# A graph-attention layer: 128 instead of 84 edge groups without gathers, in tiles of 128 consecutive edges, their column one-hots made by ScalarE

## The chip, the core and the metric

The kernel runs on one core of a Trainium2 chip. The metric is device microseconds of one execution; beside it there is one profiled execution, to which all times of single instructions belong. In the profile PE is the matrix engine (PEld its weight loads), DVE the vector engine, ACT the scalar engine (ScalarE), POOL the engine that issues indirect gathers, and SP the queue for most other DMAs.

## The reference, cut to what matters

There are 12500 nodes with 64 features and 400000 edges with 64 features, sorted by destination. Every node takes a softmax over its incoming edges and sums their messages:

```
h_src, h_dst = x[src], x[dst]
e     = leaky_relu(concat[h_src, h_dst, edge] @ W_attn + b_attn, 0.01)
alpha = exp(e - segment_max(e, dst)[dst]) / segment_sum(exp(..), dst)[dst]
z     = segment_sum(alpha * (concat[h_src, edge] @ W_ne), dst)
out   = layernorm(x + relu(concat[x, z] @ W_out))
```

The destination of the edge at place e of the sorted list is about 12500 (e/400000)², so low-numbered nodes have many edges each, and a run of consecutive edges there touches few nodes.

## The kernel before, in words

Because W_ne is linear, the kernel sums alpha-weighted raw features (`acc`, 128 x nodes: 64 rows for edge features, 64 for source features) and multiplies by the weights once per node.

Edges come in 782 groups of 512 (`GE`), a group being 128 partitions x 4 places (`P`, `T`). Edge number 4p + t of a group lies in partition p and place t.

**Main loop** (L717 to L748). Groups 83 to 781 go through batches of 20 groups (`BS`; the last two have 11 and 8), each of chunks of four groups (`SG`). For a chunk, `gather` (L176) loads the edge features with one DMA on SP and the source rows with 16 indirect DMAs on POOL (L191), into one of eight buffers (`ZB`). `scores` (L197) makes the attention scores on DVE; ScalarE copies each chunk's window of destination terms to `win` (L205, one buffer). `softmax` (L271) is a chain of scans and transposes, nearly all on DVE, at whose end ScalarE stores the weights in `fixed` (L354). `aggregate` (L366) weighs one-hots of the destinations (`w`, L369, DVE), multiplies features by them on PE (L377), 64 matmul instructions per chunk, and adds each group's 48-node window to `acc` (L387, DVE). Only when a chunk's matmuls are done is its buffer free for the gathers of a later chunk.

**Dense part** (`dense_part`, L548). The first 84 groups (`KD`), where edges crowd on few nodes, take no gathers. It is a generator: each `yield` ends one *step*, and the main loop calls one step after each chunk's scores and one after every second chunk's aggregation (`i % 2`, L742). The groups come in three dense batches of 32, 28 and 24 (`DENSE`), and for each of these:

- Set-up: two steps. `indices` (L128) loads and transposes sources and destinations (`lo` and `hi` are source modulo 128 and source divided by 128; `drel` the destination relative to the group's first).
- Score steps (L585 to L607), one per group: PE spreads the low source numbers over the partitions, DVE turns them into a one-hot `lot` (L593), PE multiplies it with the table of source scores (L596), and DVE picks with a one-hot of `hi` (L598 to L606).
- The dense softmax (L611) and a step's end.
- Aggregation steps (L621 to L645), one per group. For each of the four places DVE makes `lo_w`, a 128 x 128 one-hot of the low source number times alpha (L628), and `hot_c`, a one-hot of the *code* (node offset x 98 + hi) over 3, 4 or 5 nodes of 98 columns (L631). PE multiplies them into one PSUM tile over the four places (L633) and the edge features by `we` (L636). Then DVE loads a register with the group's offset (L638) and adds the result to `sums` (30 nodes x 98 columns, L642) and to `esum` (L644).
- At the end of a *sub-block* of groups (`subs`): 98 matmuls of x by columns of `sums` (L658) with 25 loads of x, in five pauses, and the add to `acc_d`. There are eight sub-blocks; each begins by clearing `sums` (L618).

`finish` (L508) makes 512 finished output rows. While the dense part runs, it is called only after the aggregation of a chunk that has no step; later in the score loop too. There is also a general path, started when a flag (`odd`, `worst`) says that a window was too narrow; it isn't run for this input.

PSUM tile `pg` has four buffers, which matmul results of the main loop, of the dense part and of `finish` share. Each engine runs its instructions in order; the order is settled when the program is built, and follows the program closely.

Of the kernel before, what the change touches and what calls it, by code (L numbers as in the profile page):

```python
# [9 lines left out]
F32 = mybir.dt.float32  # L10
I32 = mybir.dt.int32
# [4 lines left out]
P = 128  # L16
# [18 lines left out]
DENSE = ((32, 3, (32,)), (28, 4, (10, 9, 9)), (24, 5, (7, 6, 6, 5)))  # L35
KD = 84
ND = 5
NA = 30
NDW = 192
# [7 lines left out]
def sorted_path(ctx, tc, x, dst, idx, edge, w_ne, w_attn, b_attn, w_out, out, flag):  # L47

# [46 lines left out]
    ofs = const.tile([1, KD], I32, name="ofs")  # L95
# [32 lines left out]
    def indices(g0, G, dense=False):  # L128
# [13 lines left out]
        if dense:  # L142
            low = dn.tile([P, T, P], F32, name="lot", bufs=2).bitcast(I32)
            nc.vector.tensor_scalar(low[0:G], raw[0:G].rearrange("g (p c) -> g c p", c=2 * T)[:, 0:T, :],
                                    P - 1, None, op0=OP.bitwise_and)
            lows = chunks.tile([BG, T, P], BF16, name="lows", bufs=1)
            nc.scalar.activation(lows[0:G], low[0:G], AF.Copy)
        nat = raw.bitcast(F32)
# [5 lines left out]
        pp = psum.tile([P, 2 * T, BG], F32, name="pp", bufs=1)  # L154
# [3 lines left out]
        srcs = chunks.tile([P, T, BG], I32, name="srcs_d" if dense else "srcs", bufs=1 if dense else 3)  # L158
# [3 lines left out]
        return (srcs, pp, lows) if dense else (srcs, pp)  # L162

    def slots_of(g0, G, pp, wide=S, name="drel", bufs=3):

        drel = chunks.tile([P, T, BG], F32, name=name, bufs=bufs)
        nc.scalar.activation(drel[:, :, 0:G], pp[:, T:2 * T, 0:G], AF.Copy)
# [103 lines left out]
    def softmax(G, y, d3, carry, first, alpha=alpha, tag=""):  # L271
# [25 lines left out]
        er = rows.tile([P, T, P // T], F32, name="er")  # L297
        nc.vector.transpose(er.rearrange("r t q -> r (t q)"), y.rearrange("p t g -> p (t g)"))
        e = rows.tile([P, P], F32, name="e")
        nc.scalar.activation(e.rearrange("r (q t) -> r q t", t=T), er.rearrange("r t q -> r q t"), AF.Copy)  # L300
# [37 lines left out]
        else:  # L338
# [11 lines left out]
        nc.vector.tensor_tensor(al.rearrange("r t q -> r q t"), ex.rearrange("r (q t) -> r q t", t=T),  # L350
                                sm.rearrange("r (q t) -> r q t", t=T), op=OP.mult)
        alpha0 = rows.tile([P, P], F32, name="b1").rearrange("p (t g) -> p t g", t=T)
        nc.vector.transpose(alpha0.rearrange("p t g -> p (t g)"), al.rearrange("r t q -> r (t q)"))
        nc.scalar.activation(alpha, alpha0, AF.Copy)  # L354
# [77 lines left out]
    with before:  # L432
# [28 lines left out]
        d0f = pre.tile([1, KD], F32, name="d0f", bufs=1)  # L461
        rel = pre.tile([1, KD], F32, name="rel", bufs=1)
        nc.vector.tensor_copy(d0f, d0i[:, 0:KD])
        g0 = 0
        for n in [n for _, _, subs in DENSE for n in subs]:
            nc.vector.tensor_scalar(rel[:, g0:g0 + n], d0f[:, g0:g0 + n], d0f[:, g0:g0 + 1], None, op0=OP.subtract)
            g0 += n
        nc.vector.tensor_reduce(odd[:, 0:1], rel, axis=AX.X, op=OP.max)
        nc.vector.tensor_scalar(odd[:, 0:1], odd[:, 0:1], float(ND - NA), None, op0=OP.add)
        nc.vector.tensor_scalar(rel, rel, 0.0, float(NA - ND), op0=OP.max, op1=OP.min)  # L470
        nc.vector.tensor_copy(ofs, rel)
        nc.vector.tensor_reduce(odd[:, 1:2], d0f, axis=AX.X, op=OP.max)
        nc.vector.tensor_scalar(odd[:, 1:2], odd[:, 1:2], float(NA - NDW), None, op0=OP.add)
        nc.vector.tensor_scalar(d0f, d0f, float(NDW - NA), None, op0=OP.min)
        nc.vector.tensor_copy(at0, d0f)
# [71 lines left out]

    def dense_part():  # L548
# [5 lines left out]
        for G, wide, subs in DENSE:  # L554
            srcs, pp, lows = indices(b0, G, True)
            drel = slots_of(b0, G, pp, wide, "drel_d", 1)
# [8 lines left out]
            code = dn.tile([P, T, BG], F32, name="code")  # L565
            nc.vector.scalar_tensor_tensor(code[:, :, 0:G], drel[:, :, 0:G], float(NB), hi[:, :, 0:G], op0=OP.mult, op1=OP.add)
# [6 lines left out]
            hot = dn.tile([P, T, BG, ND], BF16, name="hot_d")  # L573
            we = dn.tile([P, T, BG, ND], F32, name="we")
            yd = dn.tile([P, T, BG], F32, name="yd")
            sdst = dn.tile([P, T, BG], F32, name="sdst_d")
            for t in range(T):
                nc.vector.tensor_tensor(hot[:, t, 0:G, :], fixed2[:, 0:ND].unsqueeze(1).to_broadcast([P, G, ND]),
                                        drel[:, t, 0:G].unsqueeze(2).to_broadcast([P, G, ND]), op=OP.is_equal)
                nc.vector.tensor_tensor(we[:, t, 0:G, :], hot[:, t, 0:G, :], pw[:, 0:G, :], op=OP.mult)  # L580
            nc.vector.tensor_reduce(sdst[:, :, 0:G], we[:, :, 0:G, :], axis=AX.X, op=OP.add)
# [3 lines left out]
            for g in range(G):  # L585
                ze = dn.tile([P, T, D], F32, name="ze_d", bufs=3)
                nc.sync.dma_start(out=ze.rearrange("p t f -> p (t f)"),
                                  in_=edge[(b0 + g) * GE:(b0 + g + 1) * GE, :].rearrange("(p t) f -> p (t f)", t=T))
# [6 lines left out]
                for t in range(T):  # L595
# [15 lines left out]
            fac, carry = softmax(G, yd, d3, carry, b0 == 0, al, "_d")  # L611
            nc.vector.tensor_tensor(we[:, :, 0:G, :], hot[:, :, 0:G, :],
                                    al[:, :, 0:G].unsqueeze(3).to_broadcast([P, T, G, ND]), op=OP.mult)
            yield
            g1 = 0
            for n in subs:
                sums = dn.tile([P, NA, NB], F32, name="sums")
                nc.vector.memset(sums, 0.0)  # L618
                esum = dn.tile([D, NA], F32, name="esum")
# [592 lines left out]
```

## Time and profile before

| | |
|---|---|
| median of 3 runs | 5798.25 us (5794.36 to 5805.65) |
| profiled execution | 5793.67 us, of which the span 5792.0 |
| busy: PE, PEld | 1926.2 us (33%), 1420.2 us (25%) |
| busy: DVE | 2616.5 us (45%) |
| busy: ACT | 249.9 us (4%) |
| busy: POOL | 2651.7 us (46%) |
| instructions | 47177 |
| DMA | 273.32 MB in 408968 packets, 226448 of them under 512 B |

The profile page gives busy time by engine, a chain of waits followed back from the end, and groups of instructions as "line engine operation output<-input, count | busy us, mean ns of one | idle time before them and what ended it". In waits, "remote" on a single core stands for a matmul whose record is missing, and "issue" is time in which nothing that the profile shows was waited for. A windows view gives for stretches of the span the busy time of each engine with the number of instructions, then the granted PE clock, the DMA share and GB/s. A timeline line is start, duration, engine, line, operation, and in brackets the idle time before it and what ended that.

### The profile page before, as it was taken

The numbers are of one execution on the slowest core, as the hardware profiler recorded it, in microseconds if no ns is written. First come the engines' busy times: TensorE is split into PE (matmuls) and PEld (weight loads), VectorE is DVE, ScalarE is ACT, GpSimd is POOL, SyncE is SP. The second block draws the span as 40 slices with busy tenths as digits, with TensorE's granted clock in tenths as the row PEclk, the third lists the DMA queues.
The fourth block names the chain that finished last, engine by engine and source line by source line (L and its number), as shares of the span: only waits on it lengthen the run. The fifth ranks groups of instructions, "written<-read, shape, count | busy, mean of one in ns | idle before, by whom it ended". The sixth has DMA issues, their size and how long they took to land.

```text
span 5792.0 us, 47177 instructions
## 1 busy us (share of the span) xinstructions
PE 1926.2 (33%) x15668; PEld 1420.2 (25%) x15668; DVE 2616.5 (45%) x7714; ACT 249.9 (4%) x575; POOL 2651.7 (46%) x2811
## 2 busy tenths in 40 slices
PE   0122222233334223232443434423333433344423
PEld 0111222122223222221232322322222322223322
DVE  4434444434554444445544544334446434253435
ACT  0000000000000000000000000000000000000000
POOL 7444444544334555544344455544443455434441
PEclk9855555555555555555655555555555555565555
DMA  7121211111112222211121222212111222212210
GB/s 125 34 45 42 45 42 41 42 42 38 40 39 57 45 48 47 44 45 40 41 60 39 62 45 46 54 46 47 43 42 37 64 45 48 52 42 54 59 42 17
DMA packets 408968, 273.32 MB, mean 47 GB/s; under 512 B 226448, under 2 KB 363196, under 8 KB 408714
## 3 DMA queue, kind: packets, MB, share of 16 engines
q1 hardware_dynamic: 292330, 170.19, 11.4%
q0 software_dynamic: 89696, 93.36, 9.8%
q10 hardware_dynamic: 26688, 6.67, 0.7%
q8 instruction: 125, 2.05, 0.1%
q14 instruction: 129, 1.06, 0.1%
HBM read 263.31 MB, written 9.07 MB: 47 GB/s over the span
## 4 chain that ended last, share of the span: by engine, by line
issue 28%; DVE 26%; another core or an unknown queue 17%; PE 16%; POOL 8%; DMA 3%; DVEq 1%; SPq 1%; ACT 1%; ACTq 0%; POOLq 0%
POOL zx L191 8%; PE pg L377 8%; PE pg L633 4%; DVE prod L223 2%; DVE prod L209 2%; DVE hot L218 2%; DVE sdst L226 2%; DVE row L237 2%; DVE turn L247 2%; DMA ze_d<-in_x_dram 2%; DVE hot_c L631 1%; DVE y L211 1%; PE pg L658 1%; DMA zx<-table,srcs 1%
## 5 line engine op out<-in xcount | busy, mean ns | idle before, releaser
L191 POOL DMA_INDIRECT zx<-table,srcs x2716 | 2565.5, 945 | 2991.9 <-PE pg L377 1973.4
L377 PE MATMUL pg<-w,ze 128*64 128x48 f32 x5592 | 716.4, 291 | 1349.1 <-issue 767.0
L377 PEld LDWEIGHTS pg<-w,ze 128*64 128x64 f32 x5592 | 622.0, 206 | 1426.9 <-issue 1112.1
L377 PE MATMUL pg<-w,zx 128*64 128x48 f32 x5592 | 726.0, 290 | 688.8 <-issue 671.0
L377 PEld LDWEIGHTS pg<-w,zx 128*64 128x64 f32 x5592 | 625.3, 205 | 743.3 <-issue 706.0
L387 DVE TENSOR_TENSOR acc<-acc,pg 128x48 f32 x699 | 137.8, 197 | 1227.8 <-remote 608.4
L633 PE MATMUL pg<-hot_c,lot 128*128 128x294 f32 (+2 forms) x672 | 442.7, 790 | 596.6 <-DVE hot_c L631 428.9
L596 PE MATMUL pg<-ss,lot 128*128 128x98 f32 x672 | 170.3, 435 | 618.0 <-DVE lot L593 382.2
L633 PEld LDWEIGHTS pg<-hot_c,lot 128*128 128x128 f32 x672 | 166.7, 285 | 789.4 <-issue 416.0
L369 DVE TENSOR_TENSOR w<-hot,fixed 128x768 f32<-128x768 bf16 x175 | 162.8, 947 | 409.9 <-remote 273.3
L596 PEld LDWEIGHTS pg<-ss,lot 128*128 128x128 f32 x672 | 149.6, 328 | 660.5 <-DVE lot L593 412.4
L631 DVE TENSOR_SCALAR hot_c<-fixed,code 128x294 f32<-128x294 f32 (+2 forms) x336 | 203.0, 604 | 179.2 <-remote 124.6
L658 PE MATMUL pg<-sums,ze_d 128*64 128x30 f32 x1568 | 188.8, 291 | 137.8 <-DMA ze_d<-in_x_dram 79.8
L205 ACT ACTIVATE win<-wrow 128x192 f32<-128x192 f32 x175 | 58.3, 333 | 3684.4 <-DVE prod L223 3075.7
L211 DVE TENSOR_REDUCE y<-prod 128x16 f32<-128x1024 f32 x175 | 211.3, 1207 | 2.8 <-issue 1.6
L658 PEld LDWEIGHTS pg<-sums,ze_d 128*64 128x64 f32 x1568 | 174.6, 219 | 155.0 <-DMA ze_d<-in_x_dram 82.6
L209 DVE TENSOR_TENSOR prod<-ze,fixed 128x1024 f32<-128x1024 f32 x175 | 211.5, 1208 | 0.0
L642 DVE TENSOR_TENSOR sums<-sums,pg 128x294 f32 (+2 forms) x84 | 46.4, 553 | 323.0 <-remote 207.6
L605 DVE TENSOR_TENSOR sel<-hot_h,pg 128x392 f32<-128x392 bf16 x84 | 47.1, 561 | 295.4 <-remote 245.8
L593 DVE TENSOR_SCALAR lot<-pg,lane 128x512 f32<-128x512 f32 x84 | 62.5, 745 | 239.4 <-remote 238.4
L226 DVE TENSOR_REDUCE sdst<-prod 128x16 f32<-128x768 f32 x175 | 164.7, 941 | 8.4 <-remote 8.2
L223 DVE TENSOR_TENSOR prod<-hot,win 128x768 f32<-128x768 bf16 x175 | 164.9, 942 | 5.1 <-ACT xtt L523 4.9
(212 smaller groups left out, 2388.6 us busy)
## 6 DMA issues: line engine op xcount, KB each, us to landing
ze<-in_edge_dram SPq DMA_DIRECT2D x173, 512.0 KB
zx<-table,srcs POOLq DMA_INDIRECT x2716
ze_d<-in_x_dram SPq DMA_DIRECT2D x192, 128.0 KB
ze_d<-in_edge_dram SPq DMA_DIRECT2D x168, 128.0 KB
wrow<-wins SPq DMA_DIRECT2D x168, 96.0 KB
table<-xt ACTq DMA_DIRECT2D x14, 227.5 KB
xb<-in_x_dram ACTq DMA_DIRECT2D x24, 128.0 KB
out_dram<-sq SPq DMA_DIRECT2D x24, 128.0 KB
```

The source lines that it names most:

```text
L191: nc.gpsimd.indirect_dma_start(out=zx[:, g, t, 0:D] if plain else zx[:, g, t, :], out_offset=None, in_=x[:, :] if plain else table[:, :], ...
L209: nc.vector.tensor_tensor(prod[:, 0:n], ze[:, 0:n], w_edge.unsqueeze(1).to_broadcast([P, n, T, D]), op=OP.mult)
L211: nc.vector.tensor_reduce(yb, prod[:, 0:n], axis=AX.X, op=OP.add)
L223: nc.vector.tensor_tensor(at[:, 0:n], hot[:, 0:n], win[:, 0:n].unsqueeze(2).to_broadcast([P, n, T, S]), op=OP.mult)
L226: nc.vector.tensor_reduce(sdst[:, 0:n], at[:, 0:n], axis=AX.X, op=OP.add)
L369: nc.vector.tensor_tensor(w[:, 0:n], hot[:, 0:n], alpha[:, :, b:b + n].rearrange("p t g -> p g t").unsqueeze(3).to_broadcast([P, n, T, S]) ...
L377: nc.tensor.matmul(pg[at:at + D, g, :], z[:, g, t, 0:D], w[:, g, t, :], start=(t == 0), stop=(t == T - 1))
L387: nc.vector.tensor_tensor(ag, ag, pg[:, g, :], op=OP.add)
L596: nc.tensor.matmul(ps[:, t, :], lot[:, t, :], ss, start=True, stop=True)
L631: nc.vector.tensor_scalar(hot_c[:, 0:wide * NB], fixed2[:, 0:wide * NB], code[:, t, g:g + 1], None, op0=OP.is_equal)
L633: nc.tensor.matmul(pa[:, 0:wide * NB], lo_w[:, t, :], hot_c[:, 0:wide * NB], start=(t == 0), stop=(t == T - 1))
L658: nc.tensor.matmul(pf[D:P, 0:NA], xb[:, j, :], sums[:, :, c0 + j], start=(c0 + j == 0), stop=(c0 + j == NB - 1))
```

## The change

- The dense part takes 128 groups rather than 84, in four dense batches of 32; the main loop keeps 655 groups (before 699) in batches of 16, then 31 of 20, then 11 and 8. The dense accumulator covers 392 nodes rather than 192. There are 16 sub-blocks rather than 8.
- In the dense part a tile (place t) now holds 128 consecutive edges: edge number 128 t + p. Its nodes span at most 2 (first two batches) or 3. Each tile has its own offset into `sums` (`ofs` has 4 per group). The loads of the edge features go in pieces of 256 bytes instead of 1024.
- `hot_c` is 2 x 98 or 3 x 98 wide, and ScalarE makes it in two activations: the distance |column − code|, then relu(1 − distance).
- Each tile has its own matmul result and its own add into `sums`: four adds of 196 or 294 columns per group rather than one of 294, 392 or 490. Four registers are loaded per group rather than one. `we` is made per group in two small DVE operations instead of once per dense batch.
- The dense softmax turns its 128 x 128 blocks with PE instead of DVE and copies.
- A sub-block's 98 matmuls have two pauses rather than five.
- The main loop calls a dense step after every chunk's aggregation rather than after every second, and in the score loop one extra step at every fourth; so `finish` isn't called while the dense part runs.

The diff, cut to its core:

```diff
-DENSE = ((32, 3, (32,)), (28, 4, (10, 9, 9)), (24, 5, (7, 6, 6, 5)))
-KD = 84
-ND = 5
+DENSE = ((32, 2, (32,)), (32, 2, (13, 10, 9)), (32, 3, (7, 7, 6, 6, 6)), (32, 3, (5, 5, 5, 5, 4, 4, 4)))
+KD = 128
+ND = 8
+NT = 3
 NA = 30
-NDW = 192
+NDW = 392
...
-    ofs = const.tile([1, KD], I32, name="ofs")
+    ofs = const.tile([1, KD * T], I32, name="ofs")
...
+        if tiles:
+            pe = psum.tile([P, SG, P], F32, name="pg", bufs=4)[:, 0, :]
+            nc.tensor.transpose(pe, y.rearrange("p t g -> p (t g)"), ident)
+            nc.scalar.activation(e, pe, AF.Copy)
...
+            nc.vector.tensor_scalar(code[:, :, 0:G], code[:, :, 0:G], -1.0, None, op0=OP.mult)
...
-                nc.sync.dma_start(out=ze.rearrange("p t f -> p (t f)"),
-                                  in_=edge[(b0 + g) * GE:(b0 + g + 1) * GE, :].rearrange("(p t) f -> p (t f)", t=T))
+                nc.sync.dma_start(out=ze, in_=edge[(b0 + g) * GE:(b0 + g + 1) * GE, :].rearrange("(t p) f -> p t f", p=P))
...
                 for g in range(g1, g1 + n):
...
+                    we = dn.tile([P, T, ND], F32, name="we")
+                    nc.vector.tensor_tensor(we, fixed2[:, 0:ND].unsqueeze(1).to_broadcast([P, T, ND]),
+                                            drel[:, :, g:g + 1].to_broadcast([P, T, ND]), op=OP.is_equal)
+                    nc.vector.tensor_tensor(we, we, al[:, :, g:g + 1].to_broadcast([P, T, ND]), op=OP.mult)
+                    _, vs = nc.values_load_multi_w_load_instructions(
+                        ofs[0:1, (b0 + g) * T:(b0 + g + 1) * T], engines=(EngineType.DVE,), min_val=0, max_val=NA - NT,
...
                     for t in range(T):
                         nc.vector.tensor_scalar(lo_w[:, t, :], fixed2[:, 0:P], lo[:, t, g:g + 1], al[:, t, g:g + 1],
                                                 op0=OP.is_equal, op1=OP.mult)
-                        hot_c = dn.tile([P, ND * NB], F32, name="hot_c", bufs=2)
-                        nc.vector.tensor_scalar(hot_c[:, 0:wide * NB], fixed2[:, 0:wide * NB], code[:, t, g:g + 1], None,
-                                                op0=OP.is_equal)
-                        nc.tensor.matmul(pa[:, 0:wide * NB], lo_w[:, t, :], hot_c[:, 0:wide * NB],
-                                         start=(t == 0), stop=(t == T - 1))
+                        hot_c = dn.tile([P, NT * NB], F32, name="hot_c", bufs=2)
+                        nc.scalar.activation(hot_c[:, 0:wide * NB], fixed2[:, 0:wide * NB], AF.Abs, bias=code[:, t, g:g + 1])
+                        nc.scalar.activation(hot_c[:, 0:wide * NB], hot_c[:, 0:wide * NB], AF.Relu, bias=one_col, scale=-1.0)
+                        pa = psum.tile([P, 512], F32, name="pg", bufs=4)
+                        nc.tensor.matmul(pa[:, 0:wide * NB], lo_w[:, t, :], hot_c[:, 0:wide * NB], start=True, stop=True)
...
+                        part = sums[:, ds(vs[t], wide), :]
+                        nc.vector.tensor_tensor(part, part, pa[:, 0:wide * NB].rearrange("l (d h) -> l d h", h=NB), op=OP.add)
...
-                    if c0 % (5 * NBC) == 4 * NBC:
+                    if c0 // NBC in (8, 16):
                         yield
...
-        def step():
-            if next(rest, done) is done:
-                return False
+        def step(n):
+            for _ in range(n):
+                if next(rest, done) is done:
+                    return False
             return True
...
                 if k and running:
-                    running = step()
                     steps += 1
+                    running = step(1 + (steps % 4 == 0))
...
-                if k and running and i % 2:
-                    running = step()
-                    steps += 1
+                if k and running:
+                    running = step(1)
```

## The prediction

> **What bounds the kernel now.** I read the page first, then the chain and the waits, then the moment at which each batch's softmax weights are stored, and last the windows between two such moments.
>
> ```profile
> PE 1926.2 (33%) x15668; PEld 1420.2 (25%) x15668; DVE 2616.5 (45%) x7714; ACT 249.9 (4%) x575; POOL 2651.7 (46%) x2811
> ...
> issue 28%; DVE 26%; another core or an unknown queue 17%; PE 16%; POOL 8%; DMA 3%; DVEq 1%; SPq 1%; ACT 1%; ACTq 0%; POOLq 0%
> ...
> L191 POOL DMA_INDIRECT zx<-table,srcs x2716 | 2565.5, 945 | 2991.9 <-PE pg L377 1973.4
> ```
>
> No engine is half busy, so stages alternate. POOL's gathers wait 1973 us for the aggregation's matmuls to free buffers. The stores of the weights give the length of a batch (start and duration come first in each line):
>
> ```profile
> 530.79 0.28 ACT L354 ACTIVATE fixed<-b 128x128 f32<-128x128 f32 x1 [9.96 <-DVE fac L363]
> 689.45 0.28 ACT L354 ACTIVATE fixed<-b 128x128 f32<-128x128 f32 x1 [9.97 <-DVE fac L363]
> 1188.66 0.28 ACT L354 ACTIVATE fixed<-b 128x128 f32<-128x128 f32 x1 [9.37 <-DVE fac L363]
> 1362.88 0.28 ACT L354 ACTIVATE fixed<-b 128x128 f32<-128x128 f32 x1 [9.96 <-DVE fac L363]
> 1885.95 0.28 ACT L354 ACTIVATE fixed<-b 128x128 f32<-128x128 f32 x1 [6.28 <-DVE fac L363]
> 2026.78 0.28 ACT L354 ACTIVATE fixed<-b 128x128 f32<-128x128 f32 x1 [9.97 <-DVE fac L363]
> ```
>
> The first pair holds seven dense score steps: 158.7 us. The second holds seven dense aggregation steps: 174.2. The third holds only light steps (x matmuls, set-up): 140.8. Of the seven steps, five lie in the score loop and two between the chunks of the aggregation. The windows show which of them cost time (length, then busy us of PE, PEld, DVE, ACT, POOL with their counts):
>
> ```profile
> 531.80:634.80 103.00, 26.91 (x339) 22.97 (x339) 19.65 (x55) 0.33 (x1) 63.44 (x68) 0.55 0.23 51
> 634.80:670.00 35.20, 12.28 (x44) 9.30 (x44) 33.94 (x69) 1.34 (x4) 12.11 (x13) 0.50 0.24 43
> ...
> 1189.40:1295.00 105.60, 34.15 (x352) 25.59 (x352) 19.16 (x57) 0.33 (x1) 63.25 (x67) 0.55 0.23 49
> 1295.00:1341.00 46.00, 23.98 (x70) 13.00 (x70) 38.22 (x84) 1.34 (x4) 12.28 (x13) 0.57 0.16 33
> ...
> 1886.60:1988.00 101.40, 34.23 (x342) 28.11 (x342) 23.22 (x59) 3.13 (x6) 63.02 (x67) 0.53 0.23 49
> ```
>
> Lines 1, 3 and 5 are aggregation phases: 101 to 106 us whatever lies in them, DVE 19 to 23 us busy. Lines 2 and 4 are score phases: DVE is busy 96% and 83% of them, and every step there lengthens the batch. The aggregation phase follows the gathers:
>
> ```profile
> 4504.26 0.94 POOL L191 DMA_INDIRECT zx<-table,srcs  x1 [3.39 <-PE pg L633]
> ...
> 4527.16 0.94 POOL L191 DMA_INDIRECT zx<-table,srcs  x1 [3.24 <-remote]
> ...
> 4550.09 0.95 POOL L191 DMA_INDIRECT zx<-table,srcs  x1 [3.25 <-remote]
> ```
>
> A chunk's 16 gathers take some 20 us (23 us from one to the next, less the gap), and 3.2 to 3.4 us after them the next chunk's buffer comes free, with or without a dense step between. So a dense step in the aggregation phase has been nearly free, one in the score loop has its price in DVE time.
>
> **The change part by part.** The base is the profiled execution, 5793.67 us (span 5792.0 and 1.7 around it), 4.6 under the median of 5798.25.
>
> *Batches.* 44 groups leave the main loop (699 to 655): 34 batches of 20 become 31 of 20 and a first of 16, and the two short ones stay. Counted from the first weights to the last short batches there are 31 full periods rather than 33: 2 x 141 (the light pair) = −282. The first batch's four groups are a fifth of a batch, twice: one chunk less before the first weights (224 us in; about −20) and one less in its aggregation (−20): −40.
>
> *Where steps fall.* Counting the loop's calls: in score phases 59 score, 62 aggregation and 33 light steps become 68, 75 and 21; in aggregation phases 25, 22 and 15 become 60, 53 and 27. A fit through the 33 periods gives 3.4 us per score step, 5.6 per aggregation step, 4.7 per light step, 13 per dense softmax and 2.7 per output block (`finish`) in a score phase, with 5.7 us of scatter. A score step keeps its DVE work (0.745 + 0.414 + 0.412 + 0.159 + 0.554 + 0.561 + 0.552 = 3.4 us, the same as its price): 9 x 3.4 = +31.
>
> *The aggregation step.* DVE before: four `lo_w` at 0.398, four `hot_c` at 0.513 to 0.713 (mean 0.604), one add of 0.553, the edge add 0.144: 4.70 us, and a load of one register at 0.31. After: four `lo_w` 1.59; four adds of 196 or 294 columns, which are 0.36 by the slope of the rows 0.461/0.562/0.664 and 0.461, so 1.43 or 1.84; two small `we` operations, taken as twice 0.19 from the 48-column add's 0.197; edge add 0.145: 3.55 or 3.96 us. Its load fetches four registers rather than one; the main loop's load of four takes 0.965. So DVE falls from 5.0 to 4.5–4.9; besides, the one-hots leave a queue that was full. I take 4.9 instead of 5.6 per step, bounds 4.1 (all of the removed `hot_c`, less the adds) and 6.5 (each add waits for its own matmul). 75 x 4.9 − 62 x 5.6 = +20.
>
> *ScalarE.* Each tile has two activations. Widths 192 and 256 take 0.334 and 0.384 us here, so 196 and 294 are about 0.34 and 0.42: 2.7 to 3.4 us for a step, some eleven steps in a batch, 30 to 37 us of 170. Hidden while DVE's own 3.6 to 4 us a step last longer; if the cover goes, the price is R3's. The 43 table loads in this trace (1.283 us each) belong to exponentials and roots; I add none.
> The Trainium skill ("ScalarE: Activation LUTs", What ACT_TABLE_LOAD costs) speaks against this: an activation whose bias is a pointer takes 280 ns + 0.833 ns per element, estimated from it 0.44 and 0.53 us, a pair 0.89 to 1.05, against DVE's 0.51 to 0.71. No row here has such a bias. A step would then be bounded by ScalarE at 3.5 to 4.2 us and I would drop the −0.7 per step: 5720 would be about 5770.
>
> *Sub-blocks* go from 8 to 16, so twice the 98 matmuls and the 25 loads of x, but two pauses instead of five: 33 matmuls per step rather than 20. 21 x 4.7 x 1.65 − 33 x 4.7 = +8. The 2.5 us clear of `sums` is in these steps. *Dense softmax:* 4 rather than 3, +13; the two transposes go from DVE to PE, taken at nothing among a chain of 18 us of DVE work (0.9 of a phase of 20); bound 0 to +1 each.
>
> *Output blocks.* 24 of them come out along the way or at the end. With a step after every chunk none is made while the dense part runs; 13 then fall into score phases, where before they hid in aggregation phases. 13 at 4.5 (2.7 by the fit; 6.3 by the bare end of the kernel; middle) less 2 at 2.7: +53. Three more in the short batches and seven rather than two after the last: +43 with 6.3 each less what the tail hides.
>
> *Edge loads* in 256-byte instead of 1024-byte pieces: SP's queue issues as many loads, three buffers ahead. q1's 292330 packets took 11.4% of 16 engines, 36 ns each; a load of 512 packets is 1.2 us over 16 engines, against 20 us between steps. The 110,000 added packets raise the DMA share by 4 points on 23%. Hidden, 0; bound +0.3 us a step, +90.
> The skill ("DMA: Bandwidth & Descriptors", Specifications) asks for 512 bytes or more for line rate and so speaks against it. A doubled packet time would still be 2.4 us a load, and the sum would not move.
>
> *Stretch of the aggregation phases.* Five steps lie there rather than two, each a chain DVE–PE–DVE in DVE's queue ahead of the next chunk's `w`, and PE's matmuls for it stand before the next chunk's. 3 more aggregation steps are 48 matmuls, 3 score steps 27. Lines 1 and 3 above differ by 13 matmuls and 2.6 us: 0.2 us each, so at most 10 and 5 us a batch; the other batches with aggregation steps last 102 to 104, which gives 0.04 and 2 us. I take 2.9 a batch, nearer the many: 28 batches, +81. Bounds 0 and +280 (the chain of waits no longer hidden at all).
>
> Sum: −282 − 40 + 31 + 20 + 8 + 13 + 53 + 43 = −154, so 5640 with the aggregation phases unchanged; +81 is 5720. Against the median shown this is −1.4%.
>
> **Rivals.**
> R1, the aggregation phases stretch: the place is the gap before a chunk's first gather, 3.3 us now, which becomes 5 or more. Against it: gaps do not differ with and without a step. For it: two steps in a row with matmuls while PE waits 1438 us for "issue". It decides from (5794 − 5640)/28 = 5.5 us a batch; at ten it gives 5920.
> R2, the phases hold wholly and the aggregation step falls to its DVE time (4.3): 5640 − 75 x 0.6 = 5595.
> R3, ScalarE in order: `win` (0.33 us) waits for DVE's L223 (3075.7 us over the run, harmless so far); now up to five tiles' one-hots stand behind it, and the adds and matmuls wait for these. One wait of 2.2 us (pair 0.8, matmul 0.7, hand-overs) per aggregation step in score phases: 75 x 2.2, on 5720, gives 5885.
> R4, the change does not do what it says: a tile with more than 2 or 3 nodes sets the flag that starts the general path. Destinations follow 12500 (e/400000)², at edge 65536 1.3 nodes per 128 edges; tiles of 2 and 3 hold for this input. Thousands of us if wrong.
>
> **How the numbers follow.** Forecast as summed 0.38, R2 0.16, no change 0.05, R1 0.24, R3 0.16, R4 0.01. Faster: 0.54; the runs of before differ by 0.2%, which is what can be told from no change. The likeliest case alone spans 5660 to 5785; with R2's lower bounds (finishes at 2.7, step at 4.1) 5560 and R1 and R3 5940.
>
> **What would show it.** Periods near 166 with score steps and 175 with aggregation steps, 31 of them; aggregation phases of 103 to 108 us, gaps of 3.3 to 4; ACT busy some 640 us (250 now, and 64 x 4 x 0.68 + 64 x 4 x 0.84 for the pairs); a pair 0.68 to 0.84 us. Wrong, if aggregation phases exceed 109 us, if DVE's adds wait for ScalarE's one-hots in the score phases, or if the periods without dense steps exceed 155 because of the output blocks.

## The result and the profile after

The changed kernel takes 6014.5 us (median of 4 runs, 6009.27 to 6016.66) against 5796.3 (4 runs, 5778.7 to 5805.65): 1.038 times before, 95% interval 1.035 to 1.041. The forecast was 5720, range 5560 to 5940. Faster was forecast and it came out slower, outside the range. The profiled execution took 6009.27 us.

The page of the changed kernel, lines that answer those of before:

```profile
PE 2414.2 (40%) x17650; PEld 1801.5 (30%) x17650; DVE 2749.5 (46%) x8457; ACT 684.8 (11%) x1554; POOL 2492.2 (41%) x2635
...
DVE 23%; issue 22%; PE 20%; another core or an unknown queue 18%; POOL 8%; DMA 5%; ACT 3%; DVEq 1%; SPq 1%; ACTq 0%; POOLq 0%
...
L214 POOL DMA_INDIRECT zx<-table,srcs x2556 | 2418.1, 946 | 3319.9 <-PE pg L412 2310.4
...
L697 PE MATMUL pg<-sums,ze_d 128*64 128x30 f32 x3136 | 388.3, 291 | 357.1 <-DMA ze_d<-in_x_dram 257.3
```

160 of these gathers are gone (147 us of POOL's busy time), and so are 16 of the first batch's, which read `x` itself and are listed apart: 176, four for each of 44 groups. But POOL waits 2310 us instead of 1973 for the aggregation's matmuls. PE has 13% more matmul records, and those of x double from 1568 to 3136.

Two of the changed kernel's phases with aggregation steps, then a pair around the end of a sub-block (windows; length, then busy us and counts of PE, PEld, DVE, ACT, POOL):

```profile
872.30:975.90 103.60, 47.75 (x387) 35.77 (x388) 30.27 (x97) 16.21 (x37) 62.76 (x67) 0.52 0.21 53
975.90:1055.30 79.40, 33.69 (x110) 19.74 (x110) 54.34 (x189) 26.62 (x65) 12.90 (x14) 0.50 0.11 24
2127.00:2252.00 125.00, 55.89 (x534) 47.13 (x534) 34.17 (x81) 4.07 (x11) 61.96 (x66) 0.52 0.28 65
2252.00:2325.00 73.00, 36.38 (x117) 21.27 (x117) 43.05 (x170) 28.13 (x68) 13.69 (x15) 0.52 0.13 29
```

The first is an aggregation phase (from the weights' store to the last add into `acc`) with dense steps between all chunks: 103.6 us, no longer than before (102 to 106). The second, the scores and softmax after it, has grown to 79.4 us from 68, and DVE is idle for a third of it. The third line is an aggregation phase that holds the 98 x matmuls of a sub-block: 125 us, 534 matmul records. The fourth is the score phase behind it.

Where the steps really fall is seen by counting `lo_w` (four per aggregation step) in the same two stretches, here for that line alone (length, DVE busy, count, clock, DMA share, GB/s). Changed kernel:

```profile
872.30:975.90 103.60, 7.25 (x19) 0.52 0.21 53
975.90:1055.30 79.40, 11.49 (x29) 0.50 0.11 24
```

Kernel before:

```profile
1188.90:1295.00 106.10, 2.02 (x5) 0.55 0.22 49
1295.00:1363.00 68.00, 9.10 (x23) 0.58 0.12 26
```

In the changed kernel's score loop and softmax there are 29, that is 7.25 steps, where the loop's calls there are 6. The fifth step of the aggregation loop is called after the last chunk, so nothing of the phase is left to hide it. Before, 23 (5.75 steps) where 5 were called.

What DVE waits for in such a score loop (976 to 1035 us; engine, tile and line; waited for; us in total, times, longest):

```profile
PEld pg L675 <- ACT hot_c L673: 33.0, 19, 5.3
ACT hot_c L672 <- DVE lot L668: 28.2, 14, 6.2
DVE sums L681 <- PE pg L675: 9.6, 8, 2.7
DVE sums L681 <- PE pg L678: 5.4, 5, 1.5
```

ScalarE's Abs waits for DVE's `lo_w`, PE for ScalarE's Relu, and DVE's add into `sums` for PE. With two smaller entries DVE waits 19 us there before its adds; in the score loop of before (1295 to 1341 us) it is 7.

### The profile page after: what moved, and what is told of

Its sections match the earlier page's. It is cut to its first block, busy times and chain, and to the rows that moved or that the text cites. A ratio compares the mean times of both kernels' runs of the same rounds, so it can differ in the third digit from the quotient of the medians.

```text
span 6007.6 us, 54654 instructions
## 1 busy us (share of the span) xinstructions
PE 2414.2 (40%) x17650; PEld 1801.5 (30%) x17650; DVE 2749.5 (46%) x8457; ACT 684.8 (11%) x1554; POOL 2492.2 (41%) x2635
## 3 DMA queue, kind: packets, MB, share of 16 engines
q14 instruction: 154, 1.25, 0.1%
## 4 chain that ended last, share of the span: by engine, by line
DVE 23%; issue 22%; PE 20%; another core or an unknown queue 18%; POOL 8%; DMA 5%; ACT 3%; DVEq 1%; SPq 1%; ACTq 0%; POOLq 0%
POOL zx L214 8%; PE pg L412 7%; PE pg L675 5%; DMA ze_d<-in_x_dram 3%; PE pg L697 3%; DVE lot L668 1%; PE pg L678 1%; DVE prod L232 1%; DVE prod L246 1%; ACT hot_c L672 1%; DVE hot L241 1%; ACT hot_c L673 1%; DVE row L260 1%; DVE turn L270 1%
## 5 line engine op out<-in xcount | busy, mean ns | idle before, releaser
L214 POOL DMA_INDIRECT zx<-table,srcs x2556 | 2418.1, 946 | 3319.9 <-PE pg L412 2310.4
L675 PE MATMUL pg<-hot_c,lot 128*128 128x196 f32 (+1 forms) x1024 | 569.1, 668 | 441.7 <-ACT hot_c L673 316.3
L633 PE MATMUL pg<-ss,lot 128*128 128x98 f32 x1024 | 259.5, 434 | 750.4 <-DVE lot L630 686.4
L697 PE MATMUL pg<-sums,ze_d 128*64 128x30 f32 x3136 | 388.3, 291 | 357.1 <-DMA ze_d<-in_x_dram 257.3
L697 PEld LDWEIGHTS pg<-sums,ze_d 128*64 128x64 f32 x3136 | 355.4, 220 | 414.5 <-DMA ze_d<-in_x_dram 282.3
L675 PEld LDWEIGHTS pg<-hot_c,lot 128*128 128x128 f32 x1024 | 251.3, 302 | 660.0 <-ACT hot_c L673 530.7
L672 ACT ACTIVATE hot_c<-fixed,code 128x196 f32<-128x196 f32 (+1 forms) x512 | 238.3, 465 | 1748.0 <-DVE lot L668 1055.4
L681 DVE TENSOR_TENSOR sums<-sums,pg 128x196 f32 (+1 forms) x512 | 208.7, 408 | 286.8 <-PE pg L675 123.4
L668 DVE TENSOR_SCALAR lot<-fixed,lo,al_d 128x128 f32<-128x128 f32 x512 | 204.5, 399 | 196.0 <-ACT hot_c L672 160.6
L673 ACT ACTIVATE hot_c<-hot_c,one_col 128x196 f32<-128x196 f32 (+1 forms) x512 | 255.4, 499 | 16.0
```

Of the source, the lines that this page charges most:

```text
L214: nc.gpsimd.indirect_dma_start(out=zx[:, g, t, 0:D] if plain else zx[:, g, t, :], out_offset=None, in_=x[:, :] if plain else table[:, :], ...
L633: nc.tensor.matmul(ps[:, t, :], lot[:, t, :], ss, start=True, stop=True)
L668: nc.vector.tensor_scalar(lo_w[:, t, :], fixed2[:, 0:P], lo[:, t, g:g + 1], al[:, t, g:g + 1], op0=OP.is_equal, op1=OP.mult)
L672: nc.scalar.activation(hot_c[:, 0:wide * NB], fixed2[:, 0:wide * NB], AF.Abs, bias=code[:, t, g:g + 1])
L673: nc.scalar.activation(hot_c[:, 0:wide * NB], hot_c[:, 0:wide * NB], AF.Relu, bias=one_col, scale=-1.0)
L675: nc.tensor.matmul(pa[:, 0:wide * NB], lo_w[:, t, :], hot_c[:, 0:wide * NB], start=True, stop=True)
```

## The experiments

The recorded pair and e13 to e15 ran under a condition in which the kernel before takes 5800 us; in all other runs it takes 3600 us and the changed one 3923. The expectations speak of two chips. The record doesn't show that: the chip with number 3 stands for runs of both kinds (e1 to e8 and e16 to e18 at 3600, e13 to e15 at 5800), number 1 for e9 to e12 at 3600. Whether it is another chip or another condition of one is open. Times are therefore given as ratios to before beside it, and each experiment says what it can tell of which condition. I call them the 5800 runs and the 3600 runs.

**The two kernels in the 3600 runs (e5, e9).** No edit.

> The changed kernel itself, on the chip of these runs, beside the kernel before. The four experiments so far ran on a chip where the kernel before takes 3600 us instead of 5796, so it must be told what the changed kernel takes beside it. If the chip only scales things: 1.038 times before, some 3735 where before is 3600. But with the own column copy the ratio was 1.053, with 24 of 25 x loads left out 1.099: if both removed something, the changed kernel lies above them, 1.08 to 1.12 times before (3890 to 4030 where before is 3600). Where before is near 5800: 1.035 to 1.042.

3923.4 us against 3599.3: 1.090 (1.088 to 1.092). The loss is more than twice as large there.

> The kernel before, unchanged, to have its profile on the chip of these experiments. If that chip has PE free of the waits for 'issue' during gathers (1438 us in the first profile of before), its aggregation phases last 25 to 60 us instead of 102, and the score phases with softmax the same 55 (score steps) and 68 us (aggregation steps) as in the first profile; DVE is then over 70% busy and bounds the kernel.

3597 us. PE's matmuls wait 67 us for "issue" instead of 1438, the aggregation phases last 22 to 45 us, and DVE is 74% busy. DVE was expected to bound the kernel. But what bounds many batches is POOL, in this window of before (one batch; the last pair is POOL) and in the chain:

```profile
531.80:631.80 100.00, 30.03 (x391) 25.51 (x391) 73.10 (x207) 4.38 (x12) 75.72 (x80) 0.57 0.33 69
```

```profile
POOL 38%; DVE 23%; issue 18%; PE 12%; DMA 7%; ACT 1%; DVEq 1%; SPq 0%; POOLq 0%; ACTq 0%
```

```profile
699.98 0.94 POOL L191 DMA_INDIRECT zx<-table,srcs  x1 [0.30 <-issue]
701.23 0.94 POOL L191 DMA_INDIRECT zx<-table,srcs  x1 [0.30 <-issue]
```

80 gathers, one every 1.25 us, are exactly a batch's 100 us. By its weights' stores the changed kernel's batches with score steps last mostly 115 us there in the first half of the run and 95 to 98 in the second, those with aggregation steps alone 121 to 126: where eleven steps make a batch longer than 100 us, POOL no longer bounds it.

**ScalarE's reading of a tile that DVE reads too (e1, e15).** In the changed kernel's program every Abs waits for DVE and 383 of the 512 `lo_w` for ScalarE, though neither writes what the other reads; both read the PSUM tile `fixed2`. e1 and e15 give ScalarE a copy of its own in SBUF.

```diff
+    cols = const.tile([P, NT * NB], F32, name="cols")
...
-                        nc.scalar.activation(hot_c[:, 0:wide * NB], fixed2[:, 0:wide * NB], AF.Abs, bias=code[:, t, g:g + 1])
+                        nc.scalar.activation(hot_c[:, 0:wide * NB], cols[:, 0:wide * NB], AF.Abs, bias=code[:, t, g:g + 1])
```

> The changed kernel, but ScalarE reads the column numbers for its distances from a copy of its own in SBUF instead of from the PSUM tile fixed2, which DVE reads for lo_w. In the changed kernel's program each Abs waits for DVE and each lo_w for ScalarE, and in the trace each Abs starts 0.1 us after a lo_w ends. Theory A (this hand-over between the two readers of one PSUM tile is what made an aggregation step in the score loop 6.9 us instead of the 4.9 forecast): 75 such steps give back 1 to 2 us each, 5860 to 5940 us. Rival B (two activations of 0.46 and 0.50 us per tile with two buffers are the limit themselves): less than 30 us, 5985 to 6015. Rival C (the add after each tile's own matmul is the limit): also under 30 us.

3788.0 us, 1.053 (1.051 to 1.054): 135 us faster than the changed kernel (3923). The waits of the changed kernel (e5) and of e1 (engine, tile and line; waited for; us in total, times, longest):

```profile
ACT hot_c L672 <- DVE lot L668: 649.4, 338, 28.5
PEld pg L675 <- ACT hot_c L673: 594.6, 403, 3.2
```

```profile
ACT hot_c L676 <- PE pg L679: 611.3, 334, 19.2
...
PEld pg L679 <- ACT hot_c L677: 191.7, 165, 1.9
```

ScalarE no longer waits for `lo_w` but for the matmul that frees a buffer, ahead of time, and PE waits a third as long for it. Aggregation phases with five steps fall from 50 to 31 us, score phases with six from 75 to 68. In e1's program no `lo_w` waits for ScalarE. The instructions themselves got no shorter (`lo_w` 0.40 us in both, Abs 0.42 and 0.51 from PSUM, 0.45 and 0.54 from the copy), so the reading of the tile was not the cost; the order was. The hand-over is shown for the 3600 runs.

> The changed kernel with ScalarE's own column copy once more, in case the runs land on a chip like that of the first pair (before near 5800). There the aggregation phases last 100 us and hide what lies in them, so only the 75 aggregation steps of the score loop gain: 6.9 to about 5.9 us, 60 to 110 us, 5900 to 5955 (1.018 to 1.028 times before). Where before is 3600: 3788 again, 1.053.

In a 5800 run: 6050.4 us, 1.044 (1.041 to 1.046), not faster than the changed kernel's 1.038. The expectation fell. Score phases with six aggregation steps called are 76.6 instead of 79.5 us, so the copy saves 3 us in each, but the 13 periods with ends of sub-blocks are 40 us longer in sum (2546 against 2506). In these periods, but for 3 us, DVE waits for `win`, ScalarE's copy of a chunk's window. First the changed kernel, then e15, whole runs:

```profile
DVE prod L246 <- ACT win L228: 49.7, 6, 13.7
DVE prod L247 <- ACT win L229: 90.2, 9, 18.9
```

That is 41 us more; before there was none. In e15 at 2216 us, for instance, `win` stands in ScalarE's queue behind a one-hot that waits 19.4 us for PE, while PE is at the x matmuls and waits up to 6.7 us at a time for loads of x; DVE waits 14.9 us for that `win`. No run takes this wait away alone.

**One-hots on DVE again (e2).**

```diff
-                        nc.scalar.activation(hot_c[:, 0:wide * NB], fixed2[:, 0:wide * NB], AF.Abs, bias=code[:, t, g:g + 1])
-                        nc.scalar.activation(hot_c[:, 0:wide * NB], hot_c[:, 0:wide * NB], AF.Relu, bias=one_col, scale=-1.0)
+                        nc.vector.tensor_scalar(hot_c[:, 0:wide * NB], fixed2[:, 0:wide * NB], code[:, t, g:g + 1], None,
+                                                op0=OP.is_equal)
```

> The changed kernel with hot_c made by DVE in one comparison again (196 or 294 columns, about 0.42 and 0.51 us by the rows of before), nothing on ScalarE. DVE gets 512 x 0.46 = 236 us more work, some 60% of it under the aggregation phases' idle time. Theory A or B (ScalarE's way of making them costs more than it saves): same or faster than the changed kernel, 5930 to 6010. If ScalarE did save what was forecast (1.85 us per step in the score loop, 75 steps): 6100 to 6150.

4007.8, 1.114 (1.112 to 1.116): 84 us slower than with ScalarE, even with its hand-over. So ScalarE's part does save in the 3600 runs, 84 us as made and 220 with its own copy; theories A and B expected the contrary. The saving that was forecast for DVE, 1.85 us in 75 steps or 139 us, lies between.

**Loads of x and matmuls of x at the sub-blocks' ends (e3, e17, e4, e16, e8).** e3 loads x once per sub-block into a buffer of the edge loads; e17 once for all into a place of its own; both keep the 98 matmuls. e4 and e16 keep 4 of 98 matmuls.

```diff
e17:
-                    xb = dn.tile([P, T, D], F32, name="ze_d", bufs=3)
...
-                        nc.tensor.matmul(pf[D:P, 0:NA], xb[:, j, :], sums[:, :, c0 + j],
+                        nc.tensor.matmul(pf[D:P, 0:NA], xone[:, j, :], sums[:, :, c0 + j],
e4:
                 for c0 in range(0, NB, NBC):
+                    if c0:
+                        if c0 // NBC in (8, 16):
+                            yield
+                        continue
```

> The changed kernel, but each sub-block loads x once (128 KB) and uses that tile in all of its 98 matmuls: 24 of 25 loads are left out (the numbers of the dense nodes' source part are then not those of the layer), the matmuls stay. In the changed kernel 16 sub-blocks lengthen their batches by some 340 us in all. Theory D (the loads are it: PE waits 540 us before these matmuls for x, and SP's queue and DVE's tail memset wait with it): 200 to 320 us faster, 5700 to 5810. Rival E (392 more PE instructions in a row are it, whatever feeds them): under 80 us, 5930 to 6010.

3949.7, 1.099 (1.096 to 1.101): 26 us slower. A buffer held through the matmuls is taken from the edge loads, which may cost something; hence e17.

> The changed kernel with all 98 x matmuls per sub-block, all of them on one tile of x loaded once at the start into a place of its own: no x loads at all (the dense nodes' source part is then not that of the layer), and unlike in e3 no buffer of the edge loads is held. Theory D (the loads, with SP's queue and PE waiting for them, are most of a sub-block's end): most of e16's gain, 150 to 280 us where before is 5796, 80 to 130 where it is 3600. Rival E (PE's 196 matmul instructions in a row are): under a third of e16's gain.

3962.7, 1.101 (1.099 to 1.103): 39 us slower without any load of x. In the 3600 runs the loads are not the cost; theory D fell there. Its trace shows a wait that moved: DVE's add into `acc_d` at a sub-block's end waits 177 us (15 times) for the last x matmul, 18 in e5; in e3 it is 184. That this is why both are slower was not tested.

> The changed kernel with only the first 4 of each sub-block's 98 blocks of x loaded and multiplied; the other loads and matmuls are left out (the dense nodes' source part is incomplete). It prices the sub-blocks' ends whole: theory D and rival E both 260 to 340 us faster than the changed kernel, 5675 to 5755. If it gains under 100 us, the sub-block batches are long for another reason.

3781.0, 1.051 (1.049 to 1.054): 142 us faster. With e17 this leaves PE's 196 matmul instructions per sub-block, and what waits for them, as the cost: 9 us for each of the 16 sub-blocks.

> The changed kernel with 4 of 98 blocks of x per sub-block, as in e4 (the dense nodes' source part is incomplete), once more for the chip on which before takes 5796. By the periods of the changed kernel's profile there, batches with sub-blocks are 344 us longer than their other steps explain: 250 to 340 us faster than the changed kernel's 6014, 0.98 to 0.995 times before. If the sub-blocks' ends are not what makes these batches long: under 120 us, above 1.015 times before. Where before is 3600: 1.051 times before again.

This run too was a 3600 run: 3783.7, 1.051. What the sub-blocks cost in the 5800 runs is thus read from periods only.

> The changed kernel, with the last two 128-row blocks of x kept in a tile of their own from the start: the memset for the partial block, which stands in DVE's queue and waits for a buffer that TensorE frees (193 us of DVE waiting in the profile of the changed kernel, 15 times, up to 26 us), and one load per sub-block fall away. If DVE's wait is what the sub-blocks cost: 100 to 190 us faster than the changed kernel. If x loads and matmuls themselves are it: under 40 us.

```diff
+                    if c0 + NBC > NFULL:
+                        xb = xlast
```

3911.9, 1.086: 11 us faster. DVE's wait for the partial block's memset (193 us in the first profile of the changed kernel, 74 in e5) is nearly all idle time that costs nothing here.

**Both together (e12).** Own column copy and 4 of 98 blocks of x.

> The changed kernel with the own column copy and only the first 4 of each sub-block's 98 blocks of x (the rest of the loads and matmuls left out; the source part of the dense nodes is incomplete). Alone the two gave 135 and 142 us where before is 3600. If they are separate costs they add: 1.013 times before, 3630 to 3670. If both remove the same stall (PE's queue in which both stand): 3720 to 3780.

3633.1, 1.010 (1.008 to 1.012): 290 us, the sum 135 + 142 and 13 more. In the 3600 runs these two are separate costs and 90% of the loss of 324.

**The form of the tiles alone (e6, e18, e7, e11).** The extent and the pacing of before.

```diff
-DENSE = ((32, 2, (32,)), (32, 2, (13, 10, 9)), (32, 3, (7, 7, 6, 6, 6)), (32, 3, (5, 5, 5, 5, 4, 4, 4)))
-KD = 128
+DENSE = ((32, 2, (32,)), (28, 2, (10, 9, 9)), (24, 3, (7, 6, 6, 5)))
+KD = 84
...
-                    running = step(1 + (steps % 4 == 0))
+                    running = step(1)
...
-                if k and running:
+                if k and running and i % 2:
e11, on e7:
-                        hot_c = dn.tile([P, NT * NB], F32, name="hot_c", bufs=2)
+                        hot_c = dn.tile([P, NT * NB], F32, name="hot_c", bufs=3)
```

> The new tiles (128 consecutive edges, ScalarE's one-hots, an add per tile) with the extent of before: 84 groups in dense batches of 32, 28 and 24, eight sub-blocks with five pauses, one step after every score part and after every second aggregation. Only the form of the dense work is changed against before. Theory A (the aggregation step has become about 0.8 us dearer instead of 0.7 cheaper by hand-overs): 62 steps in the score loop, +20 to +80 us on before. My forecast's step (0.7 cheaper): -40 us. If this alone gives the whole loss, the 44 further groups cost nothing; if it gives under a third of it, the loss is in the larger extent (sub-blocks, pacing).

3683.1, 1.023 (1.022 to 1.025). The new form costs 84 us of the 324 without any more groups, about a quarter; by its expectation the rest lies in the larger extent.

> As the run before it (84 groups, new tiles), with ScalarE reading the column numbers from its own copy. Theory A: 1.0 us less per aggregation step in the score loop (six in a row went from 74 to 68 us with it on the fast chip), 60 us faster than the run before it and 0 to 60 us faster than the kernel before. Rival B or C: no difference between the two runs beyond 15 us.

3635.8, 1.010 (1.008 to 1.012): 47 us less, still 37 slower than before, where as fast or faster was expected. One batch holds more than that: the one with the second dense softmax lasts 157 us against 106 before (98.4 + 58.7 against 44.5 + 61.7). In it DVE stands 53.9 us, its longest wait of this kind in e7:

```profile
DVE srcs L183 <- DMA zx<-table,srcs: 140.5, 5, 53.9
```

It is the cast of a later batch's source numbers into `srcs`, a tile that gathers still read. In sum it waits there 75 us in before, 237 in the changed kernel and 268 in e1; no run takes it away, so what it costs is not known.

> 84 groups, new tiles, ScalarE's own column copy, and three hot_c buffers instead of two. In the trace of the changed kernel with the own copy ScalarE's Abs waits 611 us for PE's matmul to free a buffer. If that wait is on the path: 15 to 50 us faster than with two (3636 where before is 3600). If the add after each matmul is the path: within 8 us.

3632.5: 3 us. The wait for a `hot_c` buffer is not on the path of this kernel.

> The new tiles with the extent and the pacing of before, as in e6, for the chip on which before takes 5796 (where before is 3600: 1.023 again). Aggregation steps in the score phases cost about 5.2 us before and 5.7 after by the profiles, some 0.5 x 70: 20 to 60 us slower than before, 1.003 to 1.010. If the form of the tiles carried the loss there: 1.025 or more. The rest, up to the measured 1.038, is then the larger extent: twice the sub-blocks, and one of the five steps per aggregation phase that comes after its last chunk.

A 3600 run as well: 1.023, as e6. The price of the form in the 5800 runs was not measured.

**ScalarE's one-hots in the kernel before (e10).** Old tiles, one accumulated matmul.

```diff
-                        nc.vector.tensor_scalar(hot_c[:, 0:wide * NB], fixed2[:, 0:wide * NB], code[:, t, g:g + 1], None,
-                                                op0=OP.is_equal)
+                        nc.scalar.activation(hot_c[:, 0:wide * NB], cols[:, 0:wide * NB], AF.Abs, bias=code[:, t, g:g + 1])
+                        nc.scalar.activation(hot_c[:, 0:wide * NB], hot_c[:, 0:wide * NB], AF.Relu, bias=one_col, scale=-1.0)
```

> The kernel before (84 groups, tiles of 4p + t, one accumulated matmul and one add per group) with one part of the change alone: hot_c by ScalarE's Abs and Relu, from a column copy of its own in SBUF; the accumulator of a sub-block is 25 nodes wide instead of 30 to make room. DVE loses 336 x 0.604 = 203 us; ScalarE gets 294 to 490 columns twice, 0.9 to 1.4 us per tile, up to 5.6 us per step. If ScalarE's time hides: 60 to 160 us faster than before where before is 3600, 40 to 100 us where it is 5800. If ScalarE in order and the two hot_c buffers bind: within 30 us of before or slower.

3596.2, 0.999 (0.999 to 1.000). Taking 203 us of work from DVE gives nothing in this kernel, many of whose batches POOL's gathers bound in e9.

**More groups in the old form (e13, e14), 5800 runs.** Both have 25 nodes in a sub-block's accumulator; e13 also has the edit of e10.

```diff
-DENSE = ((32, 3, (32,)), (28, 4, (10, 9, 9)), (24, 5, (7, 6, 6, 5)))
-KD = 84
+DENSE = ((32, 3, (32,)), (32, 4, (13, 11, 8)), (32, 5, (8, 7, 7, 6, 4)))
+KD = 96
...
-                if k and running and i % 2:
+                if k and running and i % 2 == 0:
```

> The kernel before with 96 dense groups in three batches of 32 (nine sub-blocks), old tiles, hot_c by ScalarE from its own column copy, and three steps per aggregation phase rather than two. 48 gathers fewer: where before is 3600 its batches last 100 us, 80 gathers of 1.25 us, so 12 groups are 60 us. DVE loses the one-hots (0.6 us each) and gets 12 groups of 3.4 + 2.7 us. Theory F (before is bound by the gathers there, the changed kernel by DVE, since it gives each batch 11 steps): 30 to 60 us faster than before, 3540 to 3570. If dense steps cannot be added at all without DVE becoming the bound: 3600 to 3680. Where before is 5800: 20 to 90 us faster.

> The same 96 groups with the one-hots made by DVE as before. Theory F: DVE has 384 x 0.61 = 234 us more than in the run before it; where before is 3600 (DVE 74% busy) 10 to 60 us slower than that run. If ScalarE's part is worth nothing in this form (as with 84 groups, 3596 against 3598): within 8 us of it.

e14: 6044.5, 1.043 (1.040 to 1.045). Twelve groups more, in the form of before, make it 250 us slower: more groups, with one step per batch after the last chunk and a narrower accumulator, can lose as much as the whole change without the new tiles. Its score phases with aggregation steps last 76 to 80 us (before 68). Between the weights' stores the first batch, a short one here, is 68 us shorter than that of before; the 32 full periods behind it are 333 longer, 278 of it in score phases and 56 in aggregation phases. The third step's place fits that, but no run tells it from the narrower accumulator. e13: 5960.4, 1.028 (1.025 to 1.031), with 69 us in two of the same score phases: here ScalarE's one-hots, from a copy of their own and without an add per tile, are worth 84 us, where 10 to 60 were expected for a 3600 run. That e13 would beat before, by 20 to 90 us, fell. Beyond e10, which ties with it, no version came as low as the kernel before.

## Why the prediction was wrong

**The aggregation phase holds** (against R1, my doubt): with four or five steps of score or aggregation inside, phases of 100.5 and about 104 us. The +81 was not where I put it. R1 came only where a sub-block's end lies in the phase: the mean of the full periods after the first is 107.7 us, before 103.4, and all of that lies in such phases, of which my reckoning of the stretch said nothing; and with it came the sign of being wrong that I had named, phases over 109 us. One of three such phases in the trace of before, from 3650 to 3772 us, had already lasted 122 us.

**"In aggregation phases 25, 22 and 15 become 60, 53 and 27" failed.** These were counted as hidden. The step after the last chunk, one in five, 28 in all, is not: the phase's cover is over. I had the order of calls and did not ask which chunk each step stood behind. Six called steps in a score phase were 7.25 paid ones. Priced by periods without sub-blocks (score phase and softmax without dense steps 38 us, which is 55.6 less five steps of 3.5): a score phase with six aggregation steps called costs 41.5 more, 6.9 per called step where I had 4.9; 75 x 2.0 = +150 us. Six called score steps lengthen the score phase by 24.5, seven times 3.5; the whole batch, 162.8 less 140.7 for a bare one, grows by 22.1, or 3.7 per called step against my 3.4: 68 x 0.3 = +20.

**The aggregation step's 4.9 failed too**, for part of that. Per paid step it is 41.5/7.25 = 5.7, and before it was (68 − 38)/5.75 = 5.2: half a microsecond up, not 0.7 down. The terms for DVE were right: adds 0.357 and 0.458 (forecast 0.36 and 0.46), `we` 0.177 and 0.174 (0.19), edge add 0.148. But DVE is busy 54 of 79 us, where before it was busy 38 of the score loop's 46 and 19 of the softmax's 22: not its work but its waits grew, those of each add for its own tile's matmul first (19 us a score loop, 7 before). That wait was my upper bound of 6.5 and a named sign of being wrong; the price I took left it out. An activation took 0.424 and 0.507 (Abs) and 0.457 and 0.540 us (Relu), 0.88 and 1.05 a pair, against my 0.68 and 0.84. The estimate worked out from the Trainium skill ("ScalarE: Activation LUTs", What ACT_TABLE_LOAD costs) was 0.89 to 1.05, so it was the right one and mine, from rows without a pointer as bias, too low. On ScalarE in order (R3) I named `win` as the wait. It came, but where I hadn't looked: not 2.2 us with every aggregation step, but 50 us in all, nearly all of it at sub-blocks' ends. What the 3600 runs showed besides is the mutual wait of ScalarE and DVE over one PSUM tile, 135 us. In the 5800 runs its removal gained nothing net.

**The sub-blocks' "+8" was the largest miss.** I scaled 4.7 us per light step by its matmuls and let 27 light steps fall into aggregation phases at nothing, and reckoned the stretch from score and aggregation steps only. The 13 periods of the changed kernel with light steps are 344 us longer than the prices 140.7, 3.7 and 6.9 make them (21 us for each of 16 sub-blocks); 15 such periods of before 132 us (16 each). That is +181 over my 163. In the aggregation phase shown above that holds such an end PE has 534 instead of 387 matmul records; the phases with 90 or more records of x last 109 to 130 us. That loads of x, for which PE waits 257 us here, were not the cause was shown only in the 3600 runs, so in the 5800 runs it stays open which of loads, matmuls and the waits behind them lengthen these periods.

The sum: 5640 + 150 + 20 + 181, 13 for the first weights (217 instead of 204 us) and 11 for the end (215 instead of 204) is 6015, against 6009 in the profile. The 181 is what those periods have over the prices, so that the sum closes shows that little lies elsewhere, and not what the 181 are. The output blocks were right: 59.1 − 38 over five of them, 4.2 each for a forecast of 4.5. So the sign "periods without dense steps over 155" came (163.1 and 161.2) without a miss: five blocks at the forecast's 4.5 already make 163. The edge loads in small pieces took nothing that shows (DMA share 0.21 in an aggregation phase, before 0.22 to 0.23).

In the 3600 runs the question is another: the changed kernel trades 176 gathers, one every 1.25 us, which bound many batches, for 11 dense steps a batch, which made many of them longer than their gathers.

## What to carry to other kernels

A cover hides only what stands inside it: find for every step that is moved the instruction behind which it is called, and count in the trace, as with `lo_w` here, how many lie in which phase. Price the ends of loops (here a sub-block's matmuls) as carefully as their bodies when a change doubles their number. And ask of every queue in order what stands ahead of a short instruction that others wait for, as `win` here. Before two engines are made to read one PSUM tile, look at whether the program makes them wait for each other.

## What was not expected of the hardware

The same program takes 5796 us in some runs and 3598 in others, with gathers of the same length (945 and 950 ns). The largest difference in the profiles is in PE's matmuls while gathers run: in the 5800 runs many of them start one by one, 1 to 3 us apart, waiting for nothing that the profile shows. Timeline of before there:

```profile
562.43 0.24 PE L377 MATMUL pg<-w,zx 128*64 128x48 f32 x1 [1.86 <-issue]
565.23 0.24 PE L377 MATMUL pg<-w,ze 128*64 128x48 f32 x1 [2.56 <-issue]
```

and in the 3600 run e9:

```profile
567.13 0.34 PE L377 MATMUL pg<-w,ze 128*64 128x48 f32 x1 [20.39 <-DVE w L369]
567.13 0.34 PE L377 MATMUL pg<-w,zx 128*64 128x48 f32 x1
567.27 0.31 PE L377 MATMUL pg<-w,ze 128*64 128x48 f32 x1
```

The groups say the same for the whole run: L377's first form waited 767 us for "issue" in the first profile; in e9:

```profile
L377 PE MATMUL pg<-w,ze 128*64 128x48 f32 x5592 | 461.6, 256 | 701.6 <-DVE w L369 631.5 <-issue 67.3 <-PE pg L596 2.2
```

Instruction fetches took as long in both (1055 and 1058 ns each, 125 of them). The first profile also holds far fewer semaphore records than that of e9 (24455 against 67721 for the same program), so a wait that it calls "issue" may be one whose release was not recorded. What makes PE slow beside gathers in the 5800 runs stays open. Where it is, the same change costs 3.8%; where it isn't, 9.0%.
